# Layer 3's first four condition weight sets behind the last row scatter, the first rows on ACT's queue, and row pieces two and one in turn

## The chip, the cores and the metric

One core of a Trainium2 chip runs the whole program. The metric is the device time of one execution in microseconds, as the median of repeated runs; the spread of the runs is given beside it. The profile is that of one execution, whose own time is given too.

## The reference

Four layers work on 2048 tokens (2 x 1024) of 256 channels, all in float32. Each adds to `x` the result of a feed-forward step on a conditioned copy of `x`:

```python
x = x + _L0_ffn_ref(_L0_cond_ref(x, ...), ...)
x = x + _L1_ffn_ref(_L1_cond_ref(x, ...), ...)
x = x + _L2_ffn_ref(_L2_cond_ref(x, ...), ...)
x = x + _L3_ffn_ref(_L3_cond_ref(x, ...), ...)
```

The change touches the condition steps of layers 2 and 3, which are mixtures of experts of one form:

```python
shared = silu(xf @ w1) * (xf @ w3) @ w2           # all tokens
s = sigmoid(concat([xf, tf]) @ router_W)          # 8 experts
_, topk_idx = top_k(s + router_bias, 2)           # two experts for each token
gates = s_sel / (s_sel.sum() + 1e-9)
routed = sum over e of gates[:, e] * (gelu(xf @ W1e[e]) @ W2e[e])
out = (shared + routed) / (N_SHARED + 2)
```

An expert has two matrices of 256 x 256 (layer 2 has 1024 hidden channels in its shared part, layer 3 has 512). Only the two chosen experts count for a token, so the kernel sorts the tokens by expert.

## The kernel before

The kernel is written in a framework in which every engine (TensorE, VectorE, ScalarE or ACT, GpSimd or POOL) and the DMA-issuing queue of SyncE (SP) runs its own list of instructions in order; the framework sets the lists' order and puts in the waits between them. DMAs are issued by SP, by ACT (in order with its activations) and, where rows are gathered or scattered by index, by POOL. `_behind` fixes an order on one engine without a wait, and `_after` makes an instruction wait until others, DMAs too, are complete.

A condition step (`_cond_moe`) runs in these stages:

1. Three of four blocks of 512 tokens of the shared product (lines 1679 to 1709; the result is scaled into `ACC` by ACT on line 2308). In between, the router's logits, the top two and the ranks are worked out.
2. POOL scatters the rows of `Xt`, with their token numbers behind them, to `xbuf` in DRAM, sorted by expert: 32 scatters of 128 rows (line 404). `k.x` keeps the names of the scatters of this stage in `k.x.new`.
3. `slots(runs)`: the sorted rows are cut into slots of 128 rows that belong to one expert; at most 35 slots in layer 2 and 37 in layer 3 (`most`). The slots are split into four runs of consecutive slots, and the kernel takes the runs in turn, so that four sets of expert weights (`sets`, 2 x 256 KB each in `ring`) are in use. A slot's two products are `cph` (line 2085) and `cpo` (line 2092), with a Gelu on ACT between (line 2088). Its result goes by a scatter of POOL to `tbuf`.
4. The fourth block of the shared product, while the slots' results come back from `tbuf`.

The loads of stage 3 are what the change touches.

- Weights: `load(n)` issues the two DMAs of the n-th slot's set on SP (`_expert_load`, line 1884); if the set holds that expert already, the DMA is skipped at run time. `load(0)` to `load(3)` come first, and the visit of slot n then calls `load(n + 3)`.
- Rows of the first eight slots: one DMA of 128 rows (129 KB) each, into `xs` (the first four) or `xq`. They are turned by TensorE (`ps_cm`, line 502). `aside` puts a load on ACT's queue, behind the activation that `k.freed` names, which for these loads is the last one of the third shared block (line 2308). Rows 3, 4, 7 and 8 go that way.
- Rows of the later slots: groups of up to three slots, loaded as four pieces (96 KB for three slots, in runs of 256 bytes) into free space in `HT` and `XT`, eight groups at a time. They are turned by VectorE (line 1993). A group's token numbers (`xm`) are a load of their own on ACT's queue.
- The pace: in the visit of slot n, after the weights of slot n + 3, `Slots.more` issues `pace` = 2 of these pieces. `Series.slot` fetches what slot n + 2 lacks, and turns the rows of slot n + 1, ahead of slot n's products.

`next` is set for layer 3 alone. `len(runs) == 4` marks the slots described here; a second call with one run, for slots above `most`, is there for other inputs and is skipped with these.

Of the kernel before, what the change touches and what calls it, by code (L numbers as in the profile page):

```python
# [20 lines left out]
P = 128  # L21
# [359 lines left out]
def _after(k, inst, names):  # L381

    for n in names:
        k.tc.add_manual_dep(inst.ins, n, mybir.DependencyInfo(mybir.DependencyClass.Sync,
                                                              mybir.DependencyReason.DATA))
# [1484 lines left out]
            self.pair()  # L1870


def _expert_load(k, eid, i, to, E, always=False, only=range(3)):

    nc = k.nc

    e = nc.sync.value_load(eid[0:1, i:i + 1], min_val=0, max_val=E)
    new = {} if always else {"cond": e < E}
    e = nc.s_assert_within(e, 0, E - 1, skip_runtime_bounds_check_because="at E the load is skipped")
    for n, (t, a) in enumerate(to):  # L1880
        if n not in only:
            continue
        form = "o (p c) f -> p (o c) f" if n + 1 < len(to) else "o (c p) f -> p (o c) f"
        nc.sync.dma_start(t, a[bass.ds(e, 1)].rearrange(form, p=P), **new)
    return [t for t, _ in to]


def _runs(most, n):

    at = [0]  # L1890
    for j in range(n):
        at.append(at[-1] + (most - at[-1]) // (n - j) + ((most - at[-1]) % (n - j) > 0))
    return [range(a, b) for a, b in zip(at, at[1:])]


class Slots:
# [41 lines left out]
    def loads(self, todo):  # L1938

        k = self.k  # L1940
        for _, last, g in todo:
            lo, n = g[0], len(g)
            if not self.group[lo][1]:
                d = D if self.of is None else DR
                if len(self.xs) < 4 or not self.room:
                    self.xs[lo] = self.pool.tile([P, d], F32, name="xs", bufs=4)
                else:
                    self.xs[lo] = self.pool.tile([P, 2 * D], F32, name="xq", tag="yt", bufs=5)[:, 0:d]
                self.load(self.xs[lo], k.xbuf[lo * P:(lo + 1) * P, 0:d], len(self.xs) in (3, 4, 7, 8))
                yield  # L1950
                continue
            if self.of is not None and lo in self.part:
                a, b = self.part[lo]
                self.part = {i: r for i, r in self.part.items() if r != (a, b)}
                self.load(self.meta[:, a:b], k.xbuf[a * P:b * P, D:].rearrange("(i p) d -> p i d", p=P), True)
            if self.room:
                if len(self.held) >= len(self.room):
                    self.next = self.held.pop(0)
                    yield
                    self.next = None  # L1960
                self.held.append(last)
                self.room.append(self.room.pop(0))
                t = self.room[-1].rearrange("p (g b k) -> p g b k", b=4, k=64)
            else:
                t = self.pool.tile([P, 2, 4, 64], F32, name="xq", tag="yt", bufs=5)
            for q in range(4):
                self.load(t[32 * q:32 * q + 32, 0:n].rearrange("p g b k -> p (g b) k"),
                          k.xbuf[lo * P:(lo + n) * P, 64 * q:64 * q + 64].rearrange("(b s) k -> s b k", s=32))
                if q < 3:
                    yield  # L1970
            for j, i in enumerate(g):
                self.xs[i] = t[:, j]
            yield
# [43 lines left out]
class Series:  # L2017
# [29 lines left out]
    def slot(self, i, products, weights, soon=False, then=None):  # L2047

        n = self.ids.index(i)
        self.fetch(n + 2)  # L2050
        self.turn(n + 1)
        if self.soon:
            self.close()
        self.soon = soon
        p = products(self.xT.pop(i), *weights())
        if not self.pace:
            self.fetch(n + 3)
        self.stage(next(p))
        self.close()
        if then:  # L2060
            then()
        if self.pace:
            self.slots.more(self.pace, n)
        part = next(p)
        while part is not None:
            self.stage(part)
            self.part = part
            part = next(p)
        self.old = i, p
# [9 lines left out]
def _gelu_products(k, pool, psum):  # L2079

    nc = k.nc

    def products(xT, R1, R2):
        ph = psum.tile([P, 2, P], F32, name="cph", tag="mm")
        made = [nc.tensor.matmul(ph[:, f, :], R1[:, c, f * P:(f + 1) * P], xT[:, c, :], start=c == 0,  # L2085
                                 stop=c == 1) for f in range(2) for c in range(2)]
        h = pool.tile([P, 2, P], F32, name="ch", tag="sg")
        k.freed = nc.scalar.activation(h, ph, AF.Gelu)
        yield made
        yield None  # L2090
        po = psum.tile([P, D], F32, name="cpo", tag="o", bufs=2)
        made = [nc.tensor.matmul(po, h[:, f, :], R2[:, f, :], start=f == 0, stop=f == 1) for f in range(2)]  # L2092
        y = pool.tile([P, D], F32, name="ys", bufs=4)
        nc.vector.tensor_copy(y, po)
        yield made
        yield y
    return products
# [150 lines left out]
def _cond_moe(k, name, wr, bias, W1, W3, W2, nf, hold, R1, R2, gate_mult, final, lead, most, next=None):  # L2248

    nc, A, XT, HT, Xt, Ht = k.nc, k.A, k.XT, k.HT, k.Xt, k.Ht  # L2250
    rp, pool, psum = k.rp, k.pool, k.psum
    E, T, NS = 8, P, 39
    base = 0 if next else 8192
    w, rb = k.small[wr], k.small[bias]
    runs = _runs(most, 4)
    sets = []
# [64 lines left out]
    gate, eid, of, used = lead_.finish()  # L2321
# [4 lines left out]
    def slots(runs):  # L2326
        ids = [(r[n], j, n == 0 or len(runs) == 1) for n in range(len(runs[0])) for j, r in enumerate(runs) if n < len(r)]
        made = {}

        def load(n):  # L2330
            if n < len(ids):
                i, j, new = ids[n]
                made[n] = _expert_load(k, eid, i, sets[n % 4], E, new)

        for n in range(4):
            load(n)
        series = Series(k, by, [i for i, _, _ in ids], *((8, 8, 2) if len(runs) == 4 else (0, 2, 2)))
        for n, (i, _, _) in enumerate(ids):
            series.slot(i, _gelu_products(k, pool, psum), lambda: made.pop(n), then=n and (lambda: load(n + 3)))
        series.close()  # L2340
        return series.last

    used = nc.values_load(used[0:1, 0:1], min_val=0, max_val=NS)
    first = _shared_gate(k, psum, XT, lead, W1, slots(runs))
    with k.tc.If(used > most):  # L2345
        slots([range(most, NS)])
# [36 lines left out]
def _layer2_ffn(k):  # L2383
# [60 lines left out]
    def weights(i):  # L2444
        if i < 2:
            if i == 0:
                for j in range(2):
                    _expert_load(k, eid, j, sets[j], E, True, (0, 1))
                for j in range(2):
                    _expert_load(k, eid, j, sets[j], E, True, (2,))  # L2450
            return [t for t, _ in sets[i]]
        to = sets[i % 2] if i < MOST - 1 else sets[(i + 1) % 2]
        return _expert_load(k, eid, i, to, E, i in (0, 1, MOST - 1, MOST))
# [36 lines left out]
class Last:  # L2490
# [6 lines left out]
    E, F = 16, 512  # L2497
# [28 lines left out]
    def weights(self, ref=None):  # L2526

        k = self.k
        while len(self.w) < self.E and k.ring.n - len(k.ring.held) >= 2:
            hold = []  # L2530
            W1, W2 = (k.ring.take(1, hold).rearrange("p (c f) -> p c f", f=f) for f in (self.F, D))
            for w, n in ((W1, "L3_W1"), (W2, "L3_W2")):
                i = _wload(k.nc, w, k.A[n][len(self.w)])
                if ref is not None:
                    _behind(k, i, ref)
            self.w.append((W1, W2, hold))
# [270 lines left out]
    def run(self):  # L2807
# [72 lines left out]
        for n, i in enumerate(order):  # L2880
            xT = pool.tile([P, 2, P], F32, name="xsT", bufs=3)
            turns = []
            i_ = nc.vector.tensor_copy(xT, _channel_major(k, psum, at[i], self.ref, turns))
            if n == 0:
                self.ref = _warm(k, psum, turns[-1], 3)
                self.made = i_
                self.sum(2)
                self.sum(3)
            if i < E:
                end(i, slot(i, xT), self.b2[:, i, :])  # L2890
            else:
                end(i, group(i - E, xT), self.b2g[i - E])
                for e in range(4 * (i - E), 4 * (i - E) + 4):
                    k.ring.drop(self.w[e][2])
                self.weights()
            fetch(n + 5)
# [133 lines left out]
```

## Time and profile before

| | |
|---|---|
| median of 15 runs | 1382.29 us (1378.07 to 1386.85) |
| profiled execution, its own time | 1381.72 us |
| its span | 1380.0 us |
| granted TensorE clock, mean | 0.994 |
| TensorE busy | 1343.9 us (97%) |
| VectorE, ACT, POOL busy | 451.7, 301.8, 272.6 us |
| first slot's product to last slot's, layer 2 | 439.2 to 507 us |
| the same, layer 3 | 1148.7 to 1223 us |

Times are microseconds from the span's start. A line of the timeline has start, duration, engine, line of the kernel, operation, output and inputs, shape and count of the merged instructions, and in brackets how long the engine stood idle before it and what ended that. SPq and ACTq are the DMA issues in the instruction lists of SP and ACT; their duration is the time of issue, not of the transfer. A line of the windows has the stretch, its length, the busy time and count of PE, PEld (weight loads of TensorE), DVE (VectorE), ACT and POOL, then TensorE's granted clock, the mean busy share of the 16 DMA engines, and GB/s. The ends of matmuls are modelled.

### The profile page before, as it was taken

The page shows a single profiled execution, that of the slowest core. Times are in us where ns is not written, and L with a number is a line of the kernel's source. Part 1 is how long each engine was busy: PE and PEld are TensorE (multiplying, and loading weights), DVE is VectorE, ACT ScalarE, POOL GpSimd, SP SyncE. Part 2 cuts the span into 40 slices and gives each one's busy share as a digit, 9 for nine tenths or more (in the row PEclk, how much of TensorE's full clock was granted, in tenths as well). Part 3 has the DMA queues.
Part 4 walks back from the last instruction along what each step waited for, and adds up shares of the span by engine and source line. Part 5 has one row for each costly group of instructions (what it writes and reads, how often), then busy time and mean ns, then how long its engine had stood idle before and what let it go on. Part 6 is the DMA issues. An engine that isn't in the chain of part 4 may idle for free. (4 is left out here: it accounts for less than half of the span.)

```text
span 1380.0 us, 22773 instructions
## 1 busy us (share of the span) xinstructions
PE 1343.9 (97%) x8272; PEld 941.1 (68%) x8275; DVE 451.7 (33%) x1431; ACT 301.8 (22%) x636; POOL 272.6 (20%) x308
## 2 busy tenths in 40 slices
PE   9999999999999999999999999999999998998997
PEld 4544444654656886555599999999975557875675
DVE  3523232325512444421221111111115423458432
ACT  4212222224111122211111111111112212127222
POOL 0410001300332440053000010001000073430442
PEclk9999999999999999999999999999999999999999
DMA  9969992963313733082394557266458256648660
GB/s 308 322 227 347 358 371 75 322 120 138 107 54 86 184 99 113 1 313 81 71 350 134 182 177 238 70 222 218 157 175 288 97 166 146 173 153 281 215 228 16
DMA packets 213022, 254.72 MB, mean 185 GB/s; under 512 B 73799, under 2 KB 165583, under 8 KB 207264
## 3 DMA queue, kind: packets, MB, share of 16 engines
q1 hardware_dynamic: 183136, 210.03, 47.9%
q0 software_dynamic: 13744, 36.63, 7.3%
q10 hardware_dynamic: 16016, 6.46, 1.8%
q8 instruction: 69, 1.13, 0.3%
q14 instruction: 57, 0.47, 0.1%
HBM read 283.64 MB, written 46.82 MB: 239 GB/s over the span
## 5 line engine op out<-in xcount | busy, mean ns | idle before, releaser
L404 POOL DMA_INDIRECT tbuf<-ys,sdst x105 | 103.3, 984 | 444.6 <-ACT ys L2121 292.4
L1679 PE MATMUL spo<-ring,sa 128*128 128x256 f32 x704 | 165.0, 380 | 0.6 <-DVE sa L1709 0.5
L1679 PEld LDWEIGHTS spo<-ring,sa 128*128 128x128 f32 x704 | 132.4, 190 | 46.3 <-issue 28.5
L1709 DVE TENSOR_TENSOR sa<-ssg,spu 128x512 f32<-128x512 f32 x88 | 60.3, 686 | 237.0 <-PE spu L1696 232.2
L2114 DVE TENSOR_TENSOR fa<-fsg,fpu 128x512 f32<-128x512 f32 x62 | 42.6, 687 | 273.2 <-PE fpu L2109 273.2
L2109 PE MATMUL fpg<-xsT,ring 128*128 128x128 f32 x992 | 121.0, 275 | 0.0
L2109 PE MATMUL fpu<-xsT,ring 128*128 128x128 f32 x992 | 120.9, 275 | 0.0
L2109 PEld LDWEIGHTS fpg<-xsT,ring 128*128 128x128 f32 x992 | 118.0, 192 | 2.3 <-issue 0.8
L2109 PEld LDWEIGHTS fpu<-xsT,ring 128*128 128x128 f32 x992 | 115.8, 192 | 0.0
L2118 PE MATMUL fpo<-ring,fa 128*128 128x256 f32 x496 | 112.3, 379 | 0.0
L1705 ACT ACTIVATE ssg<-spg 128x512 f32<-128x512 f32 x88 | 52.5, 597 | 265.8 <-PE spg L1696 260.3
L2118 PEld LDWEIGHTS fpo<-ring,fa 128*128 128x128 f32 x496 | 91.9, 190 | 12.0 <-issue 0.8
L1696 PE MATMUL spg<-HT,ring 128*128 128x512 f32 x188 | 90.0, 593 | 0.6 <-PE warm L1659 0.6
L1696 PE MATMUL spu<-HT,ring 128*128 128x512 f32 x192 | 90.3, 593 | 0.3 <-PEq L2478 0.3
L2085 PE MATMUL cph<-xsT,ring 128*128 128x128 f32 x576 | 78.0, 279 | 6.2 <-DMA ring<-in_L_r 4.8
L2085 PEld LDWEIGHTS cph<-xsT,ring 128*128 128x128 f32 x576 | 75.6, 195 | 11.6 <-issue 4.9
L1696 PE MATMUL spu<-XT,ring 128*128 128x512 f32 x160 | 75.4, 593 | 0.3 <-PEq L2345 0.3
L2092 PE MATMUL cpo<-ring,ch 128*128 128x256 f32 x288 | 75.7, 387 | 0.0
L1696 PE MATMUL spg<-XT,ring 128*128 128x512 f32 x152 | 71.7, 593 | 0.0
L2113 ACT ACTIVATE fsg<-fpg 128x512 f32<-128x512 f32 x62 | 37.0, 597 | 136.4 <-PE fpg L2109 136.4
L1696 PEld LDWEIGHTS spu<-HT,ring 128*128 128x128 f32 x192 | 36.1, 190 | 44.6 <-issue 43.3
L1696 PEld LDWEIGHTS spu<-XT,ring 128*128 128x128 f32 x160 | 30.2, 190 | 37.5 <-issue 37.2
(695 smaller groups left out, 1721.6 us busy)
## 6 DMA issues: line engine op xcount, KB each, us to landing
ring<-in_L_w SPq DMA_DIRECT2D x105, 1024.0 KB
ring<-in_L_r SPq DMA_DIRECT2D x72, 512.0 KB
ring<-in_L_r SPq DMA_DIRECT2D x144, 256.0 KB
ring<-in_L_W SPq DMA_DIRECT2D x32, 512.0 KB
yt<-tbuf SPq DMA_DIRECT2D x48, 256.0 KB
XT<-in_L_r SPq DMA_DIRECT2D x16, 512.0 KB
HT<-in_L_r SPq DMA_DIRECT2D x8, 512.0 KB
XT<-in_L_w SPq DMA_DIRECT2D x4, 1024.0 KB
```

Of the source, the lines that this page charges most:

```text
L404: i = k.nc.gpsimd.indirect_dma_start(out=self.ap, out_offset=bass.IndirectOffsetOnAxis(ap=idx, axis=0), in_=rows, in_offset=None, **end)
L1679: mm = nc.tensor.matmul(po[g // 2][:, g % 2, :], a[:, g * P:(g + 1) * P], W2[:, f, :], start=f == 0 and g % 2 == 0, stop=f == nf - 1, skip ...
L1696: mm = nc.tensor.matmul(ps, W[:, c, f * P:(f + 1) * P], X[:, c, cols], start=c == 0, stop=c == 1)
L1705: k.silu = nc.scalar.activation(sg, pg, AF.Silu)
L1709: mul = nc.vector.tensor_mul(a, sg, pu)
L2085: made = [nc.tensor.matmul(ph[:, f, :], R1[:, c, f * P:(f + 1) * P], xT[:, c, :], start=c == 0, stop=c == 1) for f in range(2) for c in ra ...
L2092: made = [nc.tensor.matmul(po, h[:, f, :], R2[:, f, :], start=f == 0, stop=f == 1) for f in range(2)]
L2109: made = [nc.tensor.matmul(ps[:, j, :], W[:, c, (f0 + j) * P:(f0 + j + 1) * P], xT[:, c, :], start=c == 0, stop=c == 1) for ps, W in ((pg, ...
L2113: nc.scalar.activation(sg, pg, AF.Silu)
L2114: nc.vector.tensor_mul(a[:, f0:f0 + 4, :], sg, pu)
L2118: made = [nc.tensor.matmul(po, a[:, f, :], W2[:, f, :], start=f == 0, stop=f == 4 * nh - 1) for f in range(4 * nh)]
```

## The change

Three edits. `_expert_load` takes names in `after` for which its DMAs wait; `load(0)` to `load(3)` of layer 3 are given the last row scatter, `k.x.new[-1:]`. In `Slots.loads`, rows 1 to 4 instead of 3, 4, 7 and 8 go on ACT's queue; this holds for both layers. In `Series.slot`, `more` issues two pieces up to visit 6, then one in the odd visits and two in the even ones, in both layers.

```diff
--- before.py
+++ after.py
@@ -1870,7 +1870,7 @@
             self.pair()
 
 
-def _expert_load(k, eid, i, to, E, always=False, only=range(3)):
+def _expert_load(k, eid, i, to, E, always=False, only=range(3), after=()):
 
     nc = k.nc
 
@@ -1881,7 +1881,9 @@
         if n not in only:
             continue
         form = "o (p c) f -> p (o c) f" if n + 1 < len(to) else "o (c p) f -> p (o c) f"
-        nc.sync.dma_start(t, a[bass.ds(e, 1)].rearrange(form, p=P), **new)
+        dma = nc.sync.dma_start(t, a[bass.ds(e, 1)].rearrange(form, p=P), **new)
+        if after:
+            _after(k, dma, after)
     return [t for t, _ in to]
 
 
@@ -1946,7 +1948,7 @@
                     self.xs[lo] = self.pool.tile([P, d], F32, name="xs", bufs=4)
                 else:
                     self.xs[lo] = self.pool.tile([P, 2 * D], F32, name="xq", tag="yt", bufs=5)[:, 0:d]
-                self.load(self.xs[lo], k.xbuf[lo * P:(lo + 1) * P, 0:d], len(self.xs) in (3, 4, 7, 8))
+                self.load(self.xs[lo], k.xbuf[lo * P:(lo + 1) * P, 0:d], len(self.xs) <= 4)
                 yield
                 continue
             if self.of is not None and lo in self.part:
@@ -2060,7 +2062,7 @@
         if then:
             then()
         if self.pace:
-            self.slots.more(self.pace, n)
+            self.slots.more(1 if n > 5 and n % 2 else 2, n)
         part = next(p)
         while part is not None:
             self.stage(part)
@@ -2327,13 +2329,13 @@
         ids = [(r[n], j, n == 0 or len(runs) == 1) for n in range(len(runs[0])) for j, r in enumerate(runs) if n < len(r)]
         made = {}
 
-        def load(n):
+        def load(n, after=()):
             if n < len(ids):
                 i, j, new = ids[n]
-                made[n] = _expert_load(k, eid, i, sets[n % 4], E, new)
+                made[n] = _expert_load(k, eid, i, sets[n % 4], E, new, after=after)
 
         for n in range(4):
-            load(n)
+            load(n, k.x.new[-1:] if next and len(runs) == 4 else ())
         series = Series(k, by, [i for i, _, _ in ids], *((8, 8, 2) if len(runs) == 4 else (0, 2, 2)))
         for n, (i, _, _) in enumerate(ids):
             series.slot(i, _gelu_products(k, pool, psum), lambda: made.pop(n), then=n and (lambda: load(n + 3)))
```

## The prediction

> **What bounds the kernel now.** I read the page first, then the timeline of TensorE in the two places where the edited code runs: the routed slots of the condition step in layer 2 (438 to 510 us) and in layer 3 (1147 to 1224 us).
>
> ```profile
> PE 1343.9 (97%) x8272; PEld 941.1 (68%) x8275; DVE 451.7 (33%) x1431; ACT 301.8 (22%) x636; POOL 272.6 (20%) x308
> ```
>
> TensorE is busy for 97% of the span, so time comes or goes only where TensorE stands still or its clock falls. Layer 2, TensorE, then the queues of SP and ACT:
>
> ```profile
> 434.77 3.62 PE L1679 MATMUL spo<-ring,sa 128*128 128x256 f32 x16
> 438.22 0.63 PE L502 MATMUL ps_cm<-ident,xs 128*128 128x128 f32 x4
> 439.22 1.13 PE L2085 MATMUL cph<-xsT,ring 128*128 128x128 f32 x8 [0.37 <-DVE xm L2002]
> 441.16 0.47 PE L502 MATMUL ps_cm<-ident,xs 128*128 128x128 f32 x2 [0.81 <-DMA xs<-xbuf]
> 441.47 1.06 PE L2085 MATMUL cph<-xsT,ring 128*128 128x128 f32 x8
> ```
>
> ```profile
> 429.76 0.83 SPq L420 DMA_DIRECT2D xs<-xbuf  x2
> 438.42 0.60 ACT L2308 ACTIVATE ACC<-spo 128x512 f32<-128x512 f32 x1 [0.26 <-PE spo L1679]
> 438.87 0.81 ACTq L420 DMA_DIRECT2D xs<-xbuf  x2
> ```
>
> Rows 1 and 2 leave on SP at 429.76 and lie ready when the shared products end, so the slots begin at once. Rows 3 and 4 are on ACT's queue, where they stand behind the last activation of the shared block: issued at 438.87, the third is there at 441.16, 2.29 us later, and TensorE waits 0.81 us for it. Layer 3:
>
> ```profile
> 1143.69 3.62 PE L1679 MATMUL spo<-ring,sa 128*128 128x256 f32 x16
> 1147.60 1.07 PE L502 MATMUL ps_cm<-ident,xs 128*128 128x128 f32 x4 [0.30 <-DMA xs<-xbuf]
> 1148.71 1.13 PE L2085 MATMUL cph<-xsT,ring 128*128 128x128 f32 x8
> 1152.14 0.48 PE L502 MATMUL ps_cm<-ident,xs 128*128 128x128 f32 x2 [2.30 <-DMA xs<-xbuf]
> 1155.92 1.28 PE L2085 MATMUL cph<-xsT,ring 128*128 128x128 f32 x8
> ```
>
> ```profile
> 1108.34 7.20 SPq L1884 DMA_DIRECT2D ring<-in_L_r  x8
> 1145.45 0.83 SPq L420 DMA_DIRECT2D xs<-xbuf  x2
> 1148.22 0.85 ACTq L420 DMA_DIRECT2D xs<-xbuf  x2
> ```
>
> The four weight sets (eight DMAs) are issued at 1108 while the scatters still run; the rows follow the last scatter at 1145.45. The third row, on ACT from 1148.22, takes 3.92 us beside the pieces that SP sends meanwhile, and TensorE stands 2.30 us. What follows that is seen in the windows of 2 us (granted clock is the figure before the DMA share):
>
> ```profile
> 1152.00:1154.00 2.00, 1.85 (x11) 1.89 (x12) 0.65 (x3) 1.57 (x3) 0.00 (x0) 0.74 0.99 181
> 1154.00:1156.00 2.00, 2.00 (x7) 1.53 (x7) 0.26 (x1) 0.38 (x1) 0.00 (x0) 0.50 0.60 54
> ```
>
> With 0.91 in the next window, the clock cost (0.26 + 0.50 + 0.09) x 2 = 1.7 us. Last, slot 11 of layer 2, the largest wait inside the slots:
>
> ```profile
> 459.51 1.03 PE L2092 MATMUL cpo<-ring,ch 128*128 128x256 f32 x4
> 462.92 1.55 PE L2085 MATMUL cph<-xsT,ring 128*128 128x128 f32 x8 [2.39 <-DMA ring<-in_L_r]
> 458.38 0.83 SPq L420 DMA_DIRECT2D HT<-xbuf  x2
> 459.54 1.15 SPq L1884 DMA_DIRECT2D ring<-in_L_r  x2
> 461.77 0.45 DVE L1993 STREAM_TRANSPOSE xsT<-HT 128x256 f32<-128x256 f32 x1 [0.77 <-DMA HT<-xbuf]
> ```
>
> Its weights leave at 459.54 and are used at 462.92; its row tile, too, is only just there (461.77). The clock then is 0.87, 0.50 and 0.78 in three windows, 1.7 us again.
>
> **The change part by part.** The sum is made against the profiled execution, 1381.72 us (span 1380.0 and 1.7 around it); the median of the 15 runs is 0.6 us higher. No instruction is added; eight weight loads wait, eight row loads change queues (four in each layer, for the queue edit is not limited to layer 3), and some pieces go a visit later, also in both layers.
>
> *Layer 2, first rows on ACT.* ACT's queue is free for them from 438.87; 2.29 us later is 441.16 for the first row, and the second, issued 0.41 later (two take 0.81), comes at 441.57. Both transposes and a copy stand ahead of the first product: 0.42 us after the second row, 442.0 instead of 439.22. To the second product it is 0.98 (the spacing of a cph and its cpo, 441.47 to 442.45) and one transposition of 0.31: 443.3 instead of 441.47, **+1.8 us**. The old 0.81 us wait for row 3 is gone in this (row 3 is issued by 439.7, there by 442.0), so the gain is already taken off. All later slots follow on TensorE, so this goes to the end.
>
> *Layer 2, the clock.* TensorE now stands from 438.39 to 441.16, 2.8 us in one piece. The two pauses of 2.30 and 2.39 us were each followed by 1.7 us lost at half clock; a pause of 1.59 us (1171.27, before slot 10 of layer 3) by none. 2.8 lies on the side of the former, but two cases are few: between 0 and 1.7 I take **+1.2**. The Trainium skill (TensorE: Matmul & The Clock Gate, Part 1) puts the fall of the clock after at least one idle window of some 3.4 us, free-running; by that alone this term would be 0, and the two rows above contradict it as a minimum, since 2.3 us was enough.
>
> *Layer 3, weights behind the last scatter.* Taking the eight loads out of 1108 to 1115.5 gains nothing: TensorE does not use them before 1148.71, nothing else is queued on SP until 1145, and the scatters on POOL keep a spacing of 1.27 us during the loads as after them. At 1145.45 they cost SP 7.2 us of issue, to 1152.7; rows 5 to 8 follow (0.43 each, to 1154.4), then six pieces (2.93, to 1157.3). The fifth row is used at 1157.9 and was issued at 1146.3; now it leaves at 1153 and takes 2.3 to 3.9 us, so it is covered. The load for slot 4 needs the first slot's products in either order. The first set, first in the queue, is there before the first row; if that cover fails it belongs to the second rival.
>
> *Layer 3, first rows on ACT.* They leave at 1148.22 instead of 1145.45, and eight weight loads of 256 KB are in flight beside them. First row: 1148.22 + 2.29 = 1150.5 on quiet queues, + 3.92 = 1152.1 as the third row does now; I take the middle, 1151.3. A row is 129 KB; sharing the 190 to 250 GB/s that the windows from 1146 to 1152 show, it takes 1.1 us instead of the 0.41 between issues, so the second is 0.7 later. The third slot's product starts 0.84 + 1.29 + 2.0 = 4.1 us after the first row (first and second products as in layer 2, then a slot's 1.98). The pause of 4.0 us costs the clock's 1.7, as the one of 2.30 does now. 1151.3 + 0.7 + 4.1 + 1.7 = 1157.8 against 1155.92: **+1.9**; bounds +0.4 (1150.5, no spacing) and +5, if row loads wait for weights to land. The chain of waits of SP's queue already shows loads that wait for an unrelated load's landing (1.8 us in two waits for xm). That the Gelu table load comes earlier on ACT than its 1151.90 of now is hidden in the same chain.
>
> The Trainium skill (DMA: Bandwidth & Descriptors, "Issuing engines are not separate DMA queues") says that DMAs started by several engines run on the same 16 DMA engines and only issue time is saved. That speaks against this edit: by it the sum would lie at the upper end of that term, since rows on ACT do not escape the weights.
>
> *Two pieces and one in turn from visit seven.* Each piece left out of a visit spares SP 0.42 us. For layer 2 slot 11's weights (visit 8) go from 459.54 to 459.1. But the row tile of slot 11 is the fourth group, whose pieces fall in visits 6, 6, 7, 7; now they fall in 6, 6, 7, 8, so that the last one is issued behind those 512 KB of weights: at about 460.6 instead of 459.2. Its transposition was done at 462.2 with the old order; 1.4 later is 463.6, and the product starts there instead of at 462.92, +0.7. If instead the weights decide, 0.4 to 0.5 is gained, and with it the clock's 1.7 if the pause gets short enough. Bounds -2.2 and +0.9; I take **+0.3**, nearer the row tile's row, as that one arrives last. In layer 3 slot 10's load stands ahead of visit 7's pieces, so its 1.59 us remains; the smaller waits of slots 16 and 24 (0.65 and 0.21) may lose **0.3**. The later groups have two visits and more in hand even at three pieces in two visits, so they stay hidden; without it a late piece costs what slot 11's does.
>
> Sum: 1.8 + 1.2 + 1.9 + 0.3 - 0.3 = +4.9 us, 1386.6.
>
> **The rivals.** *A: the starts cost little.* Clock unharmed in layer 2, first row at 1150.5 in layer 3, slot 11 gains 0.5: 1.8 + 0.4 - 0.5 - 0.3 = +1.4, 1383.1. For it speaks the quiet queue of layer 2; against, 2 MB beside the rows in layer 3. *B: the weights take the rows' place as the wait.* Row loads on ACT, or the second and third sets, come out only as weights land, so slots 1 to 3 of layer 3 each wait: +5 there instead of 1.9, and 0.9 at slot 11: about +8.6, 1390.3. *C: the spared pieces clear the waits inside the slots.* If SP's queue length alone makes slots 10 to 12, 16 and 24 late, the whole of it may go: slot starts there are late by 4.5 us in layer 2 and 4.1 in layer 3, clock included. With the starts at +4.9: 1381.7 + 4.9 - 8.6 = 1378.0. It becomes faster from the point where more than 4.9 of the 8.6 go; one piece fewer before slot 11's load, 0.42 us against a wait of 2.39, speaks against. *D: nothing happens*, for instance because the rows were bound elsewhere; the wait for row 3 at 441.16 shows the opposite.
>
> **How the numbers follow.** Forecast 0.54, A 0.16, B 0.18, C 0.09, D 0.03. Low end: C and half of D lie below 1382, about 0.1; high end: B's upper half lies above 1391, about 0.1. So 1382 to 1391. A measurement of this kernel can tell some 0.2% (2.8 us) from no change: slower is the forecast and B with a little of A, 0.73; within is A and D, 0.18; faster is C, 0.09.
>
> **What would show it.** Right: in layer 2 the first ps_cm at about 441.2 with a wait for xs, and half clock after it; in layer 3 the first ps_cm between 1150.5 and 1152 and the third slot near 1158, each counted from its own shared block's end; slot 11 of layer 2 waiting on HT instead of ring. Wrong: a first row there earlier than 2 us after ACT's last activation; waits for ring in the first slots of layer 3 (B); no wait over 1 us after slot 9 (C).

## The result, and the profile after

The changed kernel takes 1398.0 us (1395.0 to 1402.3), before 1381.7 us in the runs beside it: ratio 1.0118, 95% interval 1.0106 to 1.0131. Slower was the forecast, but by 4.9 us; it is 16.3 us, and the range ended at 1391. The profiled execution takes 1398.73 us (span 1397.0), 17.0 us more than the one of before, with a mean clock of 0.987.

```profile
PE 1347.5 (96%) x8272; PEld 944.1 (68%) x8275; DVE 450.1 (32%) x1431; ACT 302.1 (22%) x636; POOL 272.8 (20%) x308
```

TensorE's busy time is only 3.6 us longer, so most of the 17 us is standing. Both programs have the same groups of TensorE instructions in the same order, so the two can be laid beside each other. Times are from the start of the last `spo` of the third shared block, or from slot to slot (start of `cph`). In these stretches the slots are counted from 1 (the third slot is the third that runs); a single slot, as slot 11 of layer 2 or slot 10 of layer 3, has the program's number, which starts at 0, as in the prediction.

| stretch | before | after | difference | predicted |
|---|---|---|---|---|
| to layer 2's last spo | 434.77 | 434.61 | -0.2 | 0 |
| from it to layer 2's third slot | 8.88 | 10.47 | +1.6 | +1.8, and +1.2 of clock |
| slots 3 to 11 | 14.97 | 14.97 | 0 | 0 |
| slots 11 to 20 | 20.38 | 22.05 | +1.7 | +0.3 |
| slot 20 to layer 3's last spo | 664.7 | 665.8 | +1.1 | 0 |
| from it to layer 3's third slot | 12.23 | 20.70 | **+8.5** | +1.9 |
| slots 3 to 10 | 13.43 | 13.62 | +0.2 | 0 |
| slots 10 to 13 | 8.25 | 12.38 | **+4.1** | 0 |
| slots 13 to 25 | 22.33 | 21.08 | -1.3 | -0.3 |
| slot 25 to the end | 180.1 | 181.4 | +1.3 | 0 |

Layer 2's start (timeline; start, duration, engine, line, names, then the idle time before and what ended it) is as forecast: the rows leave on ACT at 438.58, and TensorE waits for the first until 440.79.

```profile
438.58 1.79 ACTq L420 DMA_DIRECT2D xs<-xbuf  x4
...
440.79 0.92 PE L502 MATMUL ps_cm<-ident,xs 128*128 128x128 f32 x4 [2.56 <-DMA xs<-xbuf]
```

Layer 3's start, the same view:

```profile
1149.12 4.76 SPq L1884 DMA_DIRECT2D ring<-in_L_r  x8
...
1151.52 0.60 ACT L2310 ACTIVATE ACC<-spo 128x512 f32<-128x512 f32 x1 [0.26 <-PE spo L1679]
...
1154.19 1.77 SPq L420 DMA_DIRECT2D xq<-xbuf  x4
...
1158.19 1.80 ACTq L420 DMA_DIRECT2D xs<-xbuf  x4
...
1162.41 1.13 PE L502 MATMUL ps_cm<-ident,xs 128*128 128x128 f32 x4 [10.93 <-DMA xs<-xbuf]
```

ACT is done with the shared block at 1152.12, and issues the first row only at 1158.19, 6.07 us later. The row is used 4.22 us after that. TensorE stands 10.93 us. What held ACT can be read from the semaphores in the trace: the transfers that SP and ACT issue share eight completion semaphores, which the framework hands out in turn, in one order over both queues; an issue waits until the transfer eight places ahead of it has landed. In this order ACT's first row stands eight places behind the last weight and uses the same semaphore: the weight's last step on it comes at 1158.09, and ACT's wait for it ends at 1158.11. In the windows the DMA engines are full meanwhile (columns: window, busy time of PE, PEld, DVE, ACT and POOL, granted clock, DMA share, GB/s):

```profile
1154.00:1156.00 2.00, 0.00 (x0) 0.00 (x0) 0.00 (x0) 0.00 (x0) 0.00 (x0) 0.50 0.98 328
1156.00:1158.00 2.00, 0.00 (x0) 0.00 (x0) 0.00 (x0) 0.00 (x0) 0.00 (x0) 0.50 1.07 374
1158.00:1160.00 2.00, 0.00 (x0) 0.00 (x0) 0.00 (x0) 0.00 (x0) 0.00 (x0) 0.50 1.28 242
```

So two causes are possible at the start: the hold, or the 2 MB of weights ahead of the rows. Slots 10 to 13, first SP's own waits (from 1146 to 1180; total, times, longest) and slot 10 before:

```profile
SPq L420 <- DMA xm<-xbuf: 1.8, 2, 1.4
...
1172.86 1.13 PE L2085 MATMUL cph<-xsT,ring 128*128 128x128 f32 x8 [1.59 <-DMA ring<-in_L_r]
```

The same after:

```profile
SPq L420 <- DMA xm<-xbuf: 4.1, 1, 4.1
```

```profile
1178.99 0.83 SPq L420 DMA_DIRECT2D HT<-xbuf  x2
...
1187.01 1.42 PE L2087 MATMUL cph<-xsT,ring 128*128 128x128 f32 x8 [2.89 <-DMA ring<-in_L_r]
```

SP stands 4.1 us until one small `xm` load of ACT's queue has landed, by the same turn (issued at 1173.71, it lands at 1178.97); everything SP issues after it is late, and slot 10 waits 2.89 us for its weights where it waited 1.59. The longer wait is 1.3 of the 4.1 us; the rest is lost at half clock, which lasts 6.83 us from 1187.70 here and didn't come there in before. In layer 2 slot 11 now waits 3.27 us instead of 2.39, and its products run at half clock:

```profile
459.52 1.14 SPq L1884 DMA_DIRECT2D ring<-in_L_r  x2
...
460.71 0.46 SPq L420 DMA_DIRECT2D HT<-xbuf  x1
...
464.70 0.45 DVE L1995 STREAM_TRANSPOSE xsT<-HT 128x256 f32<-128x256 f32 x1 [2.27 <-DMA XT<-xbuf]
...
465.25 2.04 PE L2087 MATMUL cph<-xsT,ring 128*128 128x128 f32 x8 [3.27 <-DVE xm L2004]
```

The last piece of its row tile (460.71) stands behind the weights of 459.52, and the transposition follows 4 us later.

### The profile page after: what moved, and what is told of

Read it like the earlier page. It is cut to its first block, busy times and chain, and to the rows that moved or that the text cites. A ratio compares the mean times of both kernels' runs of the same rounds, so it can differ in the third digit from the quotient of the medians.

```text
span 1397.0 us, 22767 instructions
## 1 busy us (share of the span) xinstructions
PE 1347.5 (96%) x8272; PEld 944.1 (68%) x8275; DVE 450.1 (32%) x1431; ACT 302.1 (22%) x636; POOL 272.8 (20%) x308
## 5 line engine op out<-in xcount | busy, mean ns | idle before, releaser
L2087 PE MATMUL cph<-xsT,ring 128*128 128x128 f32 x576 | 81.0, 286 | 9.2 <-DMA ring<-in_L_r 3.7
L2087 PEld LDWEIGHTS cph<-xsT,ring 128*128 128x128 f32 x576 | 78.4, 202 | 15.3 <-issue 7.8
```

## The experiments

The runs fell on several chips. On some of them before takes 1401.6 to 1403.0 us instead of 1380.5 to 1381.7; ratios compare runs of one chip, and the stretches of the profiles are counted from a point within each execution. Theory T says that the hold by the turn of eight makes layer 3's start late, theory B that the bytes do.

**Each part alone.** e1: the weights' wait alone.

```diff
-            load(n)
+            load(n, k.x.new[-1:] if next and len(runs) == 4 else ())
```

> Only the wait: Layer 3's first eight weight loads start behind the last row scatter; rows 3, 4 (and 7, 8) on ACT's queue and the pieces as before. Theory T (an issue of SP's or ACT's queue is held until the transfer eight places ahead of it in their joint program order has landed): rows 1 and 2 stand behind eight weight issues on SP and behind the landing of weights 1 and 2, rows 3 and 4 on ACT's queue behind the last weight's landing; Layer 3's first ps_cm starts 7 to 10 us after its last spo (before 3.91 us, changed kernel 14.54 us), the third slot 5 to 7 us later than before; time before +6 to +8 us, Layer 2 unchanged. Rival S (the sum on record): the wait costs 0 to 1 us. Rival B (bytes: rows leave when the engine is free and share the DMA engines with 2 MB of weights): +3 to +6 us, ACT's row issues not held.

e2: the rows alone.

```diff
-                self.load(..., len(self.xs) in (3, 4, 7, 8))
+                self.load(..., len(self.xs) <= 4)
```

> Only the rows: rows 1 to 4 on ACT's queue, 5 to 8 on SP's, in Layers 2 and 3; weights and pieces as before. Theory T: Layer 2 starts as in the changed kernel (+1.6 us at its third slot); in Layer 3 the weights have long landed when the rows are issued, so ACT issues the rows within 1 us of its last activation, and the first ps_cm comes 6.5 to 8.5 us after the last spo (before 3.91 us); third slot +1.5 to +3 us. Time before +2.5 to +5 us. Rival S (the sum on record): +1.8 in Layer 2, +1.2 for its clock, +1.9 in Layer 3, +4.9 in all: the two differ only in the clock term of Layer 2. Rival B (bytes): as T here, since no weights move then.

e3: the pieces alone.

```diff
-            self.slots.more(self.pace, n)
+            self.slots.more(1 if n > 5 and n % 2 else 2, n)
```

> Only the pieces: one and two in turn from visit seven on; weights and rows as before. The sum on record has 0.0 us (+0.3 at Layer 2's slot 11, -0.3 at Layer 3's slots 16 and 24). The trace of the changed kernel speaks for more: +1.8 to +2.0 us at Layer 2's slot 11 (last piece behind that slot's weights, transposes 3 us late, multiplication at half clock), -1.2 us at Layer 3's slots 16 and 24, so +0.5 to +1 us. If Layer 3's slots 10 to 12 (+4.5 us in the changed kernel) come from the pieces too, they are late here as well and the time is before +5 us; if they come from the late start of SP's loads, they are as before.

e4: e1 and e2 together.

> Wait and rows, pieces as before. Theory T: ACT's first row issue in Layer 3 waits for the last weight to land, as in the changed kernel: issue about 6 us after ACT's last activation, first ps_cm 14 to 15 us after the last spo, third slot +8 to +9 us over the shift ahead of it; Layer 2 +1.6 us at its start and nothing at slot 11. Time before +10 us if Layer 3's slots 10 to 12 belong to the pieces, before +14 to +15 us if they follow from the late start. Rival S: +4.9 us. If the parts simply add, e4 is e1 plus e2; by T it is more than their sum in Layer 3, since alone neither puts the first row behind the last weight's landing.

Measured, on a chip with before at 1401.6 us:

| | ratio | 95% interval | last spo to third slot, layer 3 | slots 10 to 13 |
|---|---|---|---|---|
| e1 wait | 1.0030 | 1.0013 to 1.0047 | 11.44 | 11.18 |
| e2 rows | 1.0041 | 1.0025 to 1.0057 | 14.73 | 9.25 |
| e3 pieces | 1.0019 | 1.0002 to 1.0036 | 13.66 | 8.87 |
| e4 wait and rows | 1.0060 | 1.0041 to 1.0080 | 15.79 | 10.00 |

The parts are +4.2, +5.7 and +2.7 us, and e4 is +8.4, a little less than e1 plus e2, not more: theory T missed there, and in e1, where the first `ps_cm` comes 5.13 us after the last spo. e2's start is as expected (7.79 us, ACT's issue 0.3 us after it is free), its time 0.7 us above the range. e3 is between its two cases, with slots 10 to 12 not late. The reason for e1 and e4 is in the traces. On this chip TensorE stands 9.6 to 9.8 us in every kernel, at 1126 to 1140, ahead of the part that was edited (page of e3, timeline):

```profile
1136.21 1.09 ACT L1705 ACTIVATE ssg<-spg 128x512 f32<-128x512 f32 x2 [19.81 <-remote]
```

So the weights behind the scatter leave 4.10 us before the last spo in e4, against 1.25 us after it in the changed kernel, and are on their way while TensorE still works on the shared block. From SP's first issue there to the first `ps_cm` it is 13.18 us in e4 and 13.30 in the changed kernel: in these two the distance hardly differs, and the cost is what of it the shared block doesn't cover. Slots 10 to 13 are late with the weights' wait (e1, e4) and hardly without it.

**One suspected cause away.** On a chip with before at 1380.5 us. e5: the changed kernel again.

> The changed kernel again, beside e6 to e8. Both theories: as first measured, ratio 1.010 to 1.013 if the scatters end about 1.3 us after the start of the last spo as there; 1.006 to 1.010 if, as in e4, they end 4 us before it. In both cases by Theory T the first ps_cm starts 13.2 us after the first weight issue (13.29 and 13.18 us so far), whatever the shared block does.

e6: the eight late weight loads on POOL's queue, which doesn't share that turn.

```diff
-        dma = nc.sync.dma_start(t, a[bass.ds(e, 1)]..., **new)
+        dma = (nc.gpsimd if after else nc.sync).dma_start(t, a[bass.ds(e, 1)]..., **new)
```

> The changed kernel with the eight weight loads behind the scatter on POOL's queue instead of SP's: the same 2 MB at about the same time, outside the joint turn of SP's and ACT's transfers. Theory T (turn of eight): nothing of SP or ACT waits for a weight's landing, so ACT issues its first row within 1 us of its last activation and the first ps_cm starts 6.5 to 9 us after the last spo's start (14.54 us in the changed kernel); the weights themselves may then be what the first product waits for; time 3 to 6 us under e5. Rival B (2 MB of bytes ahead of the rows in the DMA engines): the rows still land only when the weights have, first ps_cm 12 us or more after the last spo, time within 2 us of e5.

e7: the `xm` loads on POOL's queue.

```diff
-                self.load(self.meta[:, a:b], k.xbuf[a * P:b * P, D:]..., True)
+                self.loaded = k.x.load(self.meta[:, a:b], k.xbuf[a * P:b * P, D:]..., k.nc.gpsimd)
```

> The changed kernel with the three small xm loads of each layer on POOL's queue instead of ACT's. Theory X (slots 10 to 12 of Layer 3 are late because SP's next load waits for an xm load's landing, 4.1 us on SP in the changed kernel): that wait is gone, slots 10 to 12 lose under 1.5 us in all instead of 4.5, time 2 to 4 us under e5; Layer 3's first rows stay late (14 us). Rival Y (slots 10 to 12 are late because everything on SP started late behind the weights): they stay 3 to 5 us late, time within 1.5 us of e5.

e8: a version, made from before, with `in (5, 6, 7, 8)` for `in (3, 4, 7, 8)`.

> A version against before: weights and pieces as before, rows 1 to 4 on SP's queue and rows 5 to 8 on ACT's. By Theory T and the trace of before: Layer 2 loses its wait for row 3 (0.8 us), Layer 3 its 2.3 us wait for row 3 and the half clock after it (1.7 us): time before -2 to -4.5 us if rows 5 to 8 arrive in time for the fifth slot (first used some 6 us after the shared block's end). Rival: row 5 takes row 3's place as the late one, waits of 1 to 2 us there, time before -1 to +1 us.

Measured: e5 1.0103 (1.0085 to 1.0122; from the first weight issue to the first `ps_cm` 13.9 us, 0.7 over what was expected), e6 1.0111 (1.0093 to 1.0130), e7 1.0074 (1.0058 to 1.0091), e8 0.9990 (0.9978 to 1.0003). e6's start:

```profile
1150.07 3.93 POOL L1884 DMA_DIRECT2D ring<-in_L_r  x6 [0.18 <-issue]
...
1150.62 6.77 ACTq L420 DMA_DIRECT2D xs<-xbuf  x4
...
1156.60 0.70 PE L502 MATMUL ps_cm<-ident,xs 128*128 128x128 f32 x2 [6.39 <-DMA xs<-xbuf]
...
1159.37 0.70 PE L502 MATMUL ps_cm<-ident,xs 128*128 128x128 f32 x2 [2.06 <-DMA xs<-xbuf]
```

The hold is gone: ACT issues at 1150.62, while its last activation (1150.25, 0.60 long) is still running. But the first row now takes 5.98 us to its use instead of 4.22, and the second comes 2.77 us later. First `ps_cm` 10.0 us after the last spo, between the two theories; third slot 19.51 us against 20.89 in e5, and no gain in time. Taking the hold away alone buys 1.4 us of this stretch: theory T falls as the main cause. (Two things keep e6 from being quite clean: the weights take longer on POOL's queue, 14.0 us from their first issue to the last landing against 9.0 in the changed kernel, and the rows stay in one turn with SP's rows and pieces, so that ACT's four issues take 6.77 us.) In e7 SP's wait for xm is gone, slots 10 to 13 take 7.34 us (e5: 10.79), layer 2's slots 11 to 20 17.75 us (e5: 20.88), and the time is 4.3 us under e5, though layer 3's start is even later (third slot 23.19 us after the last spo, 20.89 in e5). The weights land only 11.2 us after SP's first issue there; POOL sends the xm loads beside them (1146.11 to 1150.00), which may be the reason. Theory X holds, beyond its range and in layer 2 as well. e8 fell short: layer 3's third slot comes 2.2 us earlier, but the rows on ACT now stand in front of the Gelus (layer 2's third slot at 10.02 us instead of 8.88).

**Bytes away, and xm away from before.** On a chip with before at 1403.0 us. e9: the weights early as before, and the eight late loads once more for 8 of 128 partitions.

```diff
         for n in range(4):
-            load(n, k.x.new[-1:] if next and len(runs) == 4 else ())
+            load(n)
+        for n in range(4 if next and len(runs) == 4 else 0):
+            load(n, k.x.new[-1:], 8)     # t[0:8], and rows 0 to 7 of the source
```

> The changed kernel, but the four weight sets are loaded early as before, and behind the last scatter the same eight loads are made again for 8 of their 128 partitions (128 KB in all instead of 2 MB): the number and the turn of SP's and ACT's transfers stay, the bytes go. So far, counted from the start of the last spo: neither bytes nor hold (e2) first ps_cm 7.8 us and third slot 14.7 us; bytes without hold (e6) 10.0 and 19.5; both (changed kernel) 14.5 and 20.7. Theory T (the hold by the turn is the cost): the first row leaves when the last small load has landed, first ps_cm 9.5 to 11 us, third slot 16 to 17.5 us, time 3 to 5 us under the changed kernel. Theory B (the 2 MB ahead of the rows are the cost): as e2, first ps_cm 8 to 9 us, third slot 14.5 to 15.5 us, time 5 to 7 us under it.

e10: before with the edit of e7. e11: e10 with the edit of e3. e12: e10 with all row loads on SP (`False` for `in (3, 4, 7, 8)`).

> Before with the three xm loads of a layer on POOL's queue. Theory X (SP's loads stand behind the landing of xm, and that makes slot 11 of Layer 2 late): the wait there falls from 2.39 us to under 2 us and the clock stays up, so time before -2 to -4 us. Rival Y (the weights or the row tile of slot 11 are late on their own): time before -1 to +1 us, half clock after slot 11 as now.

> e10 with two pieces and one in turn from visit seven on. If the pieces cost through their own order (the last piece of slot 11's row tile is issued behind that slot's weights), the pause ahead of slot 11 in Layer 2 is 0.5 to 1.5 us longer than in e10 and the time 0.5 to 2 us over e10. If they cost only through xm (a changed turn), e11 is within 0.5 us of e10. By the sum on record (+0.3 and -0.3) also within 0.5 us.

> e10 with rows 1 to 8 all on SP's queue. By the trace of before row 3 then leaves some 2 us earlier in Layer 3 and 8 us earlier in Layer 2: the waits for row 3 (0.8 us in Layer 2, 2.3 us with 1.7 us of clock in Layer 3) go, time 2.5 to 4.5 us under e10. Rival: the rows themselves, not their issue, are slow in Layer 3 (3.9 us from issue to use beside the pieces), and row 3 is as late as before: within 1 us of e10.

Measured: e9 1.0112 (1.0095 to 1.0130), e10 0.9942 (0.9925 to 0.9960), e11 0.9947 (0.9927 to 0.9967), e12 0.9927 (0.9905 to 0.9949). In e9 the hold lasts until 5.01 us after SP's first issue instead of 9.07:

```profile
1169.41 3.65 SPq L1884 DMA_DIRECT2D ring<-in_L_r  x8
...
1174.43 3.17 ACTq L420 DMA_DIRECT2D xs<-xbuf  x4
...
1177.49 0.70 PE L502 MATMUL ps_cm<-ident,xs 128*128 128x128 f32 x2 [7.95 <-DMA xs<-xbuf]
```

Its time missed (a gain of 3 us or more over the changed kernel was expected by both theories; the ratio is about the same), since on that chip SP comes to its first issue only 3.50 us after the last spo. The stretch itself is the shorter one: 15.25 us from that issue to the third slot, 19.45 in the changed kernel. e10 to e12 gain what theory X says and more: out of SP's and ACT's turn, the small loads hold nobody. Of e10's 8 us (2 to 4 were expected), 4 are found in layer 2's slots 11 to 20 (18.16 us, 20.38 in before's profile) and layer 3's slots 10 to 13 (6.42, 8.25); where the others come from is not shown, as before was not profiled on that chip. e11 equals e10: in this arrangement the pieces cost nothing that can be measured. e12 is 1.8 us under e10, less than expected and within the noise; the waits for row 3 are gone (layer 2's third slot at 7.64 us, 8.88 in e10).

**The four corners on one chip**, with before at 1402.5 us.

> The changed kernel, as the corner with both bytes and hold. From the first issue behind the last scatter: first ps_cm 13 to 14 us, third slot's product 19.4 to 20 us (13.3 to 13.9 and 19.4 to 19.9 us so far); slot 10 to slot 13 of Layer 3 takes 10 to 12.4 us.

> As e6 (weights on POOL's queue): 2 MB of bytes, no hold. Theory B2 (the bytes make the start late, the turn of eight makes slots 10 to 13 late): third slot within 2 us of e13 and at least 3 us above e16, slot 10 to slot 13 takes 8 to 9 us, as without the edit. Theory T (the hold makes the start late): third slot at least 3 us below e13.

> As e9 (eight small loads behind the scatter): hold and turn, no bytes. Theory B2: first ps_cm 7.5 to 9 us and third slot 14.5 to 16 us after the first issue behind the scatter, that is 4 us or more under e13; slot 10 to slot 13 still takes 10 us or more. Theory T: third slot within 2 us of e13.

> As e2 (rows on ACT's queue, weights early): neither bytes nor hold. Both theories: first ps_cm 6 to 6.5 us and third slot 13 to 14 us after the first issue behind the scatter where the scatter ends 1.5 us behind the last spo's start; slot 10 to slot 13 takes 8 to 9.5 us. By B2 the four corners then read, for the third slot, bytes 4 to 5 us and hold 1 to 2 us.

The ratios are 1.0094 (1.0068 to 1.0120), 1.0077 (1.0051 to 1.0103), 1.0134 (1.0080 to 1.0189, two executions only) and 1.0031 (0.9993 to 1.0069). The stretches of these and of the earlier runs, counted from the first issue behind the last scatter at layer 3's start (SP's; in e14 POOL's, 0.6 us ahead of SP's), in us. "Bytes" is whether 2 MB of weights move there, "turn" whether eight weight loads stand in SP's and ACT's turn there:

| | bytes | turn | ACT free | first row issued | third slot | issue to third slot | slots 10 to 13 |
|---|---|---|---|---|---|---|---|
| after | yes | yes | 3.00 | 9.07 | 19.45 | 10.4 | 12.38 |
| e5 | yes | yes | 2.90 | 9.65 | 19.54 | 9.9 | 10.79 |
| e4 | yes | yes | 8.35 | 9.16 | 19.89 | 10.7 | 10.00 |
| e13 | yes | yes | 9.49 | 9.50 | 19.56 | 10.1 | 11.05 |
| e6 | yes | no | 2.94 | 2.72 | 18.20 | 15.5 | 8.33 |
| e14 | yes | no | 10.13 | 9.84 | 21.68 | 11.8 | 8.71 |
| e9 | no | yes | 0.75 | 5.01 | 15.25 | 10.2 | 10.93 |
| e15 | no | yes | 0.00 | 5.02 | 14.83 | 9.8 | 10.88 |
| e2 | no | no | 2.67 | 2.94 | 13.15 | 10.2 | 9.25 |
| e16 | no | no | 2.91 | 2.65 | 13.69 | 11.0 | 8.70 |

The start: the third slot follows ACT's first issue by 9.8 to 11 us wherever no weights are in flight at that time, and the first issue comes when ACT is free or the last late weight has landed, whichever is later: 9.0 to 9.6 us with 2 MB, 4.9 us with 128 KB. (e7, not in the table, has the weights landed at 11.2, the first row at 11.28 and the third slot at 21.77.) Without the turn the rows leave at 2.72 and need 15.5 us. So the 2 MB cost 4 to 5 us (19.45 to 15.25; 18.20 to 13.15), the hold 1.3 to 2.1 us (19.54 to 18.20; 15.25 to 13.15): theory B for the greater part. These numbers come from several chips; on the last chip alone the bytes make 4.7 us with the turn (19.56 to 14.83). On this last chip the corners decide less than intended, since in e13 the weights had landed just when ACT was free (9.49 and 9.50), and in e14 ACT was free only at 10.13; e14 passed its bound of 2 us over e13 by 0.1. Nor is its SP as early when the weights are loaded ahead: the first issue then comes 1.3 to 4.3 us after the last spo (e16, e15), and 5.2 to 5.9 us before it in e13 and e14. So in time nothing was gained by taking the bytes away on these chips (e9 1.0112; e15 1.0134 beside e13's 1.0094): what the bytes cost is shown for the stretch behind the first issue alone, and why that issue comes so much later in e15 was not tried. On the chip of the result it comes at nearly the same point in both kernels, 1.76 us after the last spo in before and 1.25 us in the changed one.

Slots 10 to 13 divide by the other column: 10.0 to 12.4 us where eight loads stand in the turn behind the scatter, with bytes or without, 7.7 to 9.3 us where they don't (e17 has the 7.7), and 6.4 to 7.4 us where xm is out of the turn (e7, e10, e11, e12, e18). SP's wait for xm goes with it: 3.5 to 5.1 us in the six profiles of the table with the turn, 1.8 to 3.0 us in before, e2, e6, e14 and e16. There the turn is the cause, not the bytes.

**The pieces, and the version, once more**, on a chip with before at 1402.0 us.

> As e3 (the pieces alone), on another chip if it falls so. By e3, time before +2 to +4 us; Layer 2's slot 11 to slot 14 takes 11.5 to 12.5 us (9.55 in before's profile) and slot 14 to 20 10.5 us (10.83), so some +2 us there; Layer 3's start as before. By the sum on record: 0.0 us, slot 11 to 14 under 10 us.

> As e12 (all rows on SP, xm on POOL's queue): by e12 time before -7 to -13 us. From its trace the parts that are of these edits: third slot of Layer 2 1.2 us earlier, slots 11 to 20 of Layer 2 0.5 us, third slot of Layer 3 2 to 4 us, slots 10 to 13 1.2 us, 5 to 7 us in all; if only these repeat, time before -5 to -7 us.

e17 (the edit of e3) measured 1.0011 (0.9995 to 1.0026): between 1 us less and 4 us more. In layer 2 slot 11 waits as in the changed kernel:

```profile
459.84 1.06 SPq L1884 DMA_DIRECT2D ring<-in_L_r  x2
...
460.95 0.47 SPq L420 DMA_DIRECT2D HT<-xbuf  x1
...
465.40 2.05 PE L2085 MATMUL cph<-xsT,ring 128*128 128x128 f32 x8 [4.09 <-DVE xm L2002]
```

Slots 11 to 14 take 11.89 us (9.55 in before's profile), slots 14 to 20 10.54 (10.83): the mechanism is shown, +2.1 us. But e1 and e2, without that edit, lose as much at slots 17 and 18 (slots 11 to 20: 22.75 and 21.99 us; 19.43 in e16, which has e2's edit on another chip), so on such chips a wait there may only be moved.

e18 (the edit of e12) measured 0.9911 (0.9889 to 0.9932), 9 to 16 us under before and the lowest ratio of all. Layer 3's start in it:

```profile
1156.89 3.62 PE L1679 MATMUL spo<-ring,sa 128*128 128x256 f32 x16
...
1158.21 1.77 SPq L420 DMA_DIRECT2D xs<-xbuf  x4
...
1160.39 0.94 PE L502 MATMUL ps_cm<-ident,xs 128*128 128x128 f32 x4
...
1164.69 1.06 PE L2085 MATMUL cph<-xsT,ring 128*128 128x128 f32 x8
```

Four rows leave on SP at once, the first is used 2.18 us later with no wait, and the third slot starts 7.80 us after the last spo (before 12.23). Layer 2's third slot comes at 7.64 us (8.88), its slots 11 to 20 take 17.80 us (20.38), slots 10 to 13 of layer 3 7.42 (8.25). These four make some 9 us, with before's profile taken on another chip. The edit beats before on the two chips where it ran (e12, e18); the changed kernel did not run on them, and the edit did not run on a chip of the prediction's kind.

## Why the prediction was right in direction and wrong in size

- **Layer 3, first rows on ACT** (+1.9, bounds +0.4 to +5; measured +8.5) is the step that failed. It let the rows leave when ACT is free and land 2.3 to 3.9 us later beside the weights. The trace has them leave at 1158.19 for an ACT free at 1152.12, when the last weight has landed. Leaving early would not have saved it either: without that hold the third slot still comes 18.20 us after the first issue (e6), against 19.54 with it (e5). What was priced too low is 2 MB of weights ahead of the rows, 4 to 5 us; the hold adds 1.3 to 2.1. The bound of +5, "if row loads wait for weights to land", named the right case and was too low as well: SP's first issue to the first row's is 9.1 us, ACT needs 3.0 of them for itself, and the remaining 6.1 us come on top of the +1.9. That the working from ACT's issue on nearly came out (9.6 us to the third slot, clock included, against 10.4) is luck in part: it counted with weights beside the rows, and by then there were none, while the half clock, priced at 1.7 us, lasted 13.65 us, from 1153.57 to 1167.22, and so went on for 4.8 us after TensorE had started again. The chain of SP's queue was quoted as a sign that loads wait for unrelated landings, and it was not followed to the place of each load in that turn.
- **Layer 3, weights behind the last scatter** (0). "The first set is there before the first row" was true and beside the point: the set is not what is waited for, the transfers behind it are. What the 2 MB do to the rows was put at 1.5 us (0.8 for the first row, the middle of the two cases, and 0.7 for the second); e9 and e6 make it 4 to 5 us.
- **Slots 10 to 13** (0; +4.1) had no term for the eight loads. They shift every later load's place in the turn; SP then stood 4.1 us for an xm load that it passes in 1.8 us (two waits) in before. e9 and e15 show it without the bytes, e7 takes it away. Half clock behind the longer wait makes most of the 4.1.
- **Layer 2, first rows on ACT** (+1.8; +1.6) was right, at a first `ps_cm` of 440.79.
- **Layer 2, the clock** (+1.2; 0 in this profile). The pause of 2.56 us passed at full clock here. Eleven profiles have rows 1 to 4 on ACT and a pause of 2.42 to 2.56 us there; three have the third slot at 10.45 to 10.57 us, and eight, with half clock behind the pause, at 11.67 to 12.06. The term was right as a mean and wrong for this execution; which executions get the half clock is not shown. The Trainium skill (TensorE: Matmul & The Clock Gate, Part 1) has the clock fall after at least one idle window of some 3.4 us; the pauses here are shorter and most of them were followed by half clock.
- **Two pieces and one** (+0.3 and -0.3). The mechanism at slot 11 was named and came about (the last piece behind the weights, the wait on the row tile); its size was +1.7 to +2.1 in the profiles, since the pause grew from 2.39 to 3.27 us and the half clock behind it from 3.41 to 6.83. Slots 13 to 25 gave -1.3. e3 and e17 leave +0.1 to +0.2%, e11 nothing.
- **Rivals.** B came nearest (rows on ACT come out only as weights land) and stopped at 1390.3: it took the same +5, and it had nothing at layer 3's slots 10 to 13. The Trainium skill's sentence that DMAs of several engines run on the same 16 engines (DMA: Bandwidth & Descriptors, "Issuing engines are not separate DMA queues") was quoted as speaking for the upper end; e6, with a queue of its own for the weights and 18.20 us to the third slot against 19.54, agrees.

The sum on record against the profile: 6.6 us are missing at layer 3's start, 4.1 at slots 10 to 13, 1.4 at layer 2's slot 11, 2.4 in two small stretches; against that, 2.4 less came at layer 2's start (-1.4, its clock above all) and at slots 13 to 25 (-1.0).

What stays open: the split between bytes and hold in the time of a whole execution; the +1.1 and +1.3 us in the two long stretches; how much the pieces cost on a chip of the prediction's kind; some 3 of the 12 us that e18 gains and half of e10's 8, since before was not profiled on those chips; and why the weights land later in e7.

## What to carry to other kernels

A load that is moved behind a late event takes its bytes and its place in the queue's turn with it: list what leaves after it on every queue that shares completion semaphores, and price each by the landing of the last byte ahead, not by the issue. Before loads are spread over two queues, see whether the small ones (here xm, 5.3 us from issue to landing in the changed kernel) hold the large ones; taking them out of the shared turn brought more here than any reordering of the large ones. A stretch that changes little, such as the 9.0 to 9.6 us from the first weight's issue to the last landing in five profiles, costs only what the work beside it doesn't cover, so the same two edits can put a third slot 8.5 us later in one execution and 3.6 in another (e4 against before).

## What the runs showed of the hardware

- On four chips TensorE stands 9.1 to 9.8 us in one piece in every profiled kernel, up to a point between 1131 and 1143, behind an activation before which ACT is idle for 17.0 to 19.9 us; in e3 (19.8) the DMA engines are at a share of 0.51 from 1126 to 1136. Single steps of SP's list, DMA issues not counted, take about 0.70 us there (in e3, 13 of 123 from 1100 to 1160 take 0.66 to 0.72); in the changed kernel as first profiled and in e5 none of 139 takes over 0.60. The cause was not tried.
- Half clock comes in blocks: in the clock records of these traces they last 3.41, 6.83, 10.24 or 13.65 us, apart from the one that the span's end cuts short, and within a trace they begin on one grid of 3.41 us (before: 463.46 and 1152.95, 202 steps apart). A pause of 1.85 us (e8, before layer 3's third slot) was followed by one, a pause of 2.56 us was not.
- 128 KB in eight loads have landed 1.3 us after the last issue has ended (e9, e15), 2 MB 4.2 to 4.8 us after it (changed kernel, e4, e5, e13).
